# One column of shift for Bs, dt, raw, one and z: where the inputs of GpSimd's products begin in a row

## The chip, the cores and the metric

The kernel runs on one core of a Trainium2 chip. The metric is the device time of one execution in microseconds; the times are medians over several runs. The engines are PE (TensorE), DVE (VectorE), ACT (ScalarE) and POOL (GpSimd); SP issues most of the DMAs.

## The reference, cut to what matters

Four layers follow one another on a tensor of 4 x 192 x 64 x 64. The change touches the first two, which hold three "mambas": layer 0 normalises, runs two mambas over the same tokens (one of them over flipped channels) and adds their outputs; layer 1 is one mamba, a depthwise convolution and an MLP. A mamba, for each image (b) of 4096 tokens, is:

```python
xz = x @ in_w.T
xc, z = jnp.split(xz, 2, axis=-1)              # 384 channels each
xc = silu(causal depthwise convolution of xc)  # 4 taps in layer 0, 3 in layer 1
dbl = xc @ x_w.T                               # dt (12), B (16), C (16)
dt = softplus(dt @ dt_w.T + dt_b)
def step(h, inp):
    dA = exp(dt_t[..., None] * A)
    h = dA * h + (dt_t * x_t)[..., None] * B_t[:, None, :]
    y = einsum('bdn,bn->bd', h, C_t)
y = (y + D * xc) * silu(z)
return y @ out_w.T
```

The state h has 384 channels x 16 states, and the recurrence runs over the 4096 tokens. Layers 2 and 3 (a convolution with computed weights, and windows multiplied by a large structured matrix, with an MLP) are not touched.

## The kernel before, in words

Everything is fp32. A *unit* is one mamba on one tile of T = 512 tokens: layer 0 has 4 images x 8 tiles x 2 mambas = 64 units, layer 1 has 32. In SBUF a tile has 128 partitions, and a *row* here is one run of 512 columns in the free dimension. ND = 3 chunks of 128 channels make the 384.

The front of a unit (`Mamba.front`, L721) makes on PE the projection xc, the convolution and dt; ACT moves the results from PSUM into tiles. In layer 0 (`convolve`, L806) the convolution is matmuls that read `raw` at taps j = 0 to 3 (L821). In layer 1 (`summed`, `sum_taps`, L834) ACT writes three scaled copies into `raw`, `one` and `xc` (L848), and POOL adds them with two additions over 3 x 512 columns (L857: xc + raw, L859: xc + one). `one` takes the same buffer as `dt`. Then ACT makes dt (L770, softplus L777), POOL makes dtx = dt * xc into `raw` (L778, 3 x 512 columns), and SP stores dt and dtx to DRAM (L783: r_dt, r_dtx). z is projected too (ACT L743 in layer 0, L742 in layer 1), and put through silu in place (L795).

The scan handles 32 channels x 16 states at a time, in 12 tiles (k) of four rows of 512. SP loads the rows of dt and dtx back, spread over the partitions (`load`, L867: dtE, dtxE, two buffers each). For each tile:

- `product` (L896): h = dtxE * B over 4 x 512 columns. For most tiles DVE does it with B in PSUM. For the tiles called *apart* (four of twelve in the first mamba of layer 0, five in the second, three in layer 1) POOL does it, with B loaded from DRAM into `Bs` (`spread_C` L877 in layer 0, `bring_B` L890 in layer 1), and the result is `h_apart`. Both are at L903.
- ACT makes dA = exp(dt * A) row by row (`decay`, L910).
- DVE runs the recurrence on each row (`step`, L916).
- POOL multiplies by C, also loaded from DRAM (`read`, L932: h * C over 4 x 512 columns, in place but for one column).
- PE sums over the states (`sum`, L942).

At the end of every four tiles DVE takes y out of PSUM; in layer 0 it multiplies by z itself (L964), in layer 1 POOL does (`gate`, L972: xc * z over 512 columns).

The order on every engine is written out by hand: `Scans` goes through the steps, and a planner of lanes (`Behind`) puts the front of the next unit and what follows the last one between them by fixed waits and costs. It depends on nothing measured at run time. Every engine works its list in order and waits on semaphores.

Where rows begin. In the built program each of these tiles begins at a multiple of 32 bytes (8 columns) of its partition, in the kernel before and after the change. So where a row begins, modulo 8 columns, follows from the slices alone. h and h_apart already hold one column more than T: their rows begin at columns 1, 514, 1027, 1540 when POOL reads them at L932, while C begins at 0. The table gives, row by row, (start of the second input - start of the first input) modulo 4 columns, that is, modulo 16 bytes:

| line | inputs | before | after |
|---|---|---|---|
| L903 | dtxE, Bs | 0 0 0 0 | 1 1 1 1 |
| L932 | h, C | 3 2 1 0 | 3 2 1 0 |
| L778, layer 0 | dt, xc | 0 0 0 | 3 2 1 |
| L778, layer 1 | dt, xc | 0 3 2 | 3 1 3 |
| L857 | xc, raw | 0 2 0 | 1 0 3 |
| L859 | xc, one | 0 1 2 | 1 3 1 |
| L972, by chunk | xc, z | 0, 0, 0 | 1, 2, 3 |
| L1476 (rows of 64; a product's sum in layer 1's tail) | x2, strip | 3 and 1 in turn | 3 and 1 in turn |

For example, dt in layer 1 has a pitch of 513 columns before, so its rows begin at 0, 513, 1026 and those of xc at 0, 512, 1024; the difference is 0, -1, -2, or 0, 3, 2 modulo 4.

Of the kernel before, what the change touches and what calls it, by code (L numbers as in the profile page):

```python
# [14 lines left out]
F32 = mybir.dt.float32  # L15
# [12 lines left out]
ND = DI // 128  # L28
# [5 lines left out]
T = 512  # L34
# [626 lines left out]
class Mamba:  # L661
# [59 lines left out]
    def front(self, xn, first, u):  # L721


        nc, K, behind = self.nc, self.taps, self.behind
        raw = self.work.tile([128, ND, K - 1 + T], F32, name="raw", bufs=1)
        if first:
            nc.gpsimd.memset(self.halo, 0.0)
        nc.gpsimd.tensor_copy(raw[:, :, 0 : K - 1], self.halo[:, :, : K - 1])  # L728

        def projected(e):  # L730
            ps = behind.bank([128, T], "ps_in")
            for k in range(2):
                nc.tensor.matmul(  # L733
                    ps, self.in_w[:, k, bass.ts(e, 128)], xn[:, k, :], start=(k == 0), stop=(k == 1)
                )
            return ps

        def project(e, to):
            ps = projected(e)
            if e >= ND and self.z_b is not None:  # L740
                bias = self.z_b[:, e - ND : e - ND + 1]
                return behind.later(lambda: nc.scalar.activation(to, ps, AF.Identity, bias=bias), name="z")  # L742
            return behind.later(lambda: nc.scalar.copy(to, ps))  # L743

        if self.summed:
            yield from self.sum_taps(raw, projected, u)
        else:
            yield from self.convolve(raw, project, u)
        xc = u["xc"]
        nc.scalar.activation(xc, xc, AF.Silu)  # L750
        yield Piece(2.6, bank=True, wait=3 if self.summed else 4, after=u["dbl_free"])
        ps = behind.bank([KX, T], "ps_x")
        for d in range(ND):
            nc.tensor.matmul(ps, self.x_w[:, d, :], xc[:, d, :], start=(d == 0), stop=(d == ND - 1))  # L754
        dbl = u["dbl"] = self.work.tile([KX, T], F32, name="dbl", bufs=2 if self.summed else 1)
        h = behind.later(lambda ps=ps: nc.scalar.copy(dbl, ps), name="x")
        halves = []
        for d in range(ND):
            yield Piece(0.85, bank=True, after=[h], wait=(1 if d else 3) if self.summed else (0 if d else 3))
            if d == 0:  # L760
                bc = u["bc"] = self.dram.tile([2 * NS, T], F32, name="r_bc", bufs=3)
                nc.sync.dma_start(bc, dbl[RK : RK + 2 * NS, :])
                dt = self.work.tile([128, ND, 1 + T if self.summed else T], F32, name="dt", bufs=1)
                dt = dt[:, :, :T]
                dtx = raw[:, :, K - 1 :]
            ps = behind.bank([128, T], "ps_dt")
            nc.tensor.matmul(ps, self.dt_w[:, bass.ts(d, 128)], dbl, start=True, stop=True)  # L767
            halves.append(
                behind.later(
                    lambda d=d, ps=ps: nc.scalar.activation(  # L770
                        dt[:, d, :], ps, AF.Identity, bias=self.dt_b[:, d : d + 1]
                    ),
                    name="dt",
                )
            )
        yield Piece(after=halves, burst=True, act=4.1)
        nc.scalar.activation(dt, dt, AF.Softplus)  # L777
        nc.gpsimd.tensor_tensor(dtx, dt, xc, ALU.mult)  # L778
        rows = []
        for i, v in enumerate((dt, dtx)):  # L780
            yield Piece(wait=1 + i)
            r = self.dram.tile([DI, T], F32, name=("r_dt", "r_dtx")[i], bufs=3)
            nc.sync.dma_start(r.rearrange("(c p) t -> p c t", p=128), v)  # L783
            rows.append(r)
        yield Piece(1.7, bank=True, after=u["z_free"], wait=0)
        u["rows"] = rows
        z = u["z"] = self.work.tile([128, ND, T], F32, name="z", bufs=2)
        made = []
        for d in range(ND):
            if d:  # L790
                yield Piece(1.7, bank=True, wait=0)
            made.append(project(ND + d, z[:, d, :]))

        def silu():
            nc.scalar.activation(z, z, AF.Silu)  # L795
            u["silu"] = True
            yield Piece()

        said = Piece(after=made, burst=True, act=4.1)
        if self.summed:  # L800
            behind.add(4, silu(), said)
        else:
            yield said
            yield from silu()
# [29 lines left out]
    def sum_taps(self, raw, projected, u):  # L834

        nc, behind = self.nc, self.behind
        halves = []
        for d in range(ND):
            yield Piece(1.7, bank=True, after=u["xc_free"], wait=AHEAD.get(f"w_in{d}", 0))
            if d == 0:  # L840
                xc = u["xc"] = self.last.tile([128, ND, T], F32, name="xc", bufs=self.xcs)
                one = self.work.tile([128, ND, 1 + T], F32, name="one", tag="dt", bufs=1)
                nc.gpsimd.tensor_copy(one[:, :, 0:1], self.halo[:, :, 2:])
            ps = projected(d)
            for j, o in enumerate((raw[:, d, 2:], one[:, d, 1:], xc[:, d, :])):

                def tap(o=o, ps=ps, d=d, j=j):
                    nc.scalar.activation(  # L848
                        o, ps, AF.Identity, scale=self.conv_w[:, d, j : j + 1], bias=self.tap_b[:, d, j : j + 1]
                    )  # L850

                h = behind.later(tap, bank=(j == 2), more=j, name="tap")
            halves.append(h)
        yield Piece(after=halves, wait=2)
        nc.gpsimd.tensor_copy(self.halo[:, :, :2], raw[:, :, T:])
        nc.gpsimd.tensor_copy(self.halo[:, :, 2:], one[:, :, T:])
        nc.gpsimd.tensor_tensor(xc, xc, raw[:, :, :T], ALU.add)  # L857
        yield Piece(wait=2)
        nc.gpsimd.tensor_tensor(xc, xc, one[:, :, :T], ALU.add)  # L859
        yield Piece(burst=True, wait=2, act=4.1)  # L860
# [16 lines left out]
    def spread_C(self, u, o):  # L877

        both = [("Bs", 0, 1)] if any(k % 2 == o for k in self.shared) and not self.summed else []
        both.insert(len(both) if self.summed else 0, ("C", NS, 1 if self.summed else 2))  # L880
        for n, at, bufs in both:
            if n == "C" and self.summed:
                yield Piece(wait=4)
            v = self.work.tile([128, T], F32, name=f"{n}{o}", bufs=bufs)
            rows = u["bc"][at + 8 * o : at + 8 * o + 8, :]
            self.nc.sync.dma_start(v, rows.unsqueeze(0).broadcast_to([16, 8, T]))
            u[n, o] = v
            yield Piece()

    def bring_B(self, u, o):  # L890
        v = self.work.tile([128, T], F32, name="Bs", bufs=1)
        rows = u["bc"][8 * o : 8 * o + 8, :]
        self.nc.sync.dma_start(v, rows.unsqueeze(0).broadcast_to([16, 8, T]))
        u["Bs", o] = v
# [224 lines left out]
def two_mambas(tc, x, gb_ap, m_ins, ex_aps, out, at_first):  # L1119
# [3 lines left out]
    with ExitStack() as ctx:  # L1123
# [105 lines left out]
        for n, u in enumerate(units):  # L1229
            following = units[n + 1] if n + 1 < len(units) else None  # L1230

            def before(i, n=n, u=u, following=following):
                if i == 0 and following:
                    load(following)
                    last = [units[n - 1]["added"]] if n else []
                    behind.add(3, norm(following, last), Piece(wait=3))
                if following:
                    behind.add(1, front(following, i), Piece(after=[following["normed"]], wait=2))

            for i in range(2):  # L1240
                stream.append(
                    (
                        mambas[i],
                        u[i],
                        u["t"] == 0,
                        lambda i=i, before=before: before(i),
                        (lambda u=u: behind.add(2, back(u), Piece())) if i else (lambda: None),
                    )
                )
# [64 lines left out]
def mamba_block(tc, x, p96, p96_ap, p128, p128_ap, m_in, ex_aps, out, sums, following):  # L1314
# [4 lines left out]
    with ExitStack() as ctx:  # L1319
# [193 lines left out]
        def before(n):  # L1513
            if n + 1 < len(units):
                behind.add(1, front(units[n + 1]), Piece())
            if n + 2 < len(units):
                behind.add(1, norm(units[n + 2]), Piece(1.7, bank=True, after=[units[n + 2]["loaded"]]))
# [857 lines left out]
```

## Time and profile before

| | us |
|---|---|
| median of 3 runs | 9663.74 (9659.62 to 9670.88) |
| the profiled execution | 9663.24 |
| its span, first to last instruction | 9661.5 |
| PE busy | 8021.0 (83%) |
| DVE busy | 8580.3 (89%) |
| ACT busy | 6529.2 (68%) |
| POOL busy | 7624.1 (79%) |

The profile is of one execution; its own time is 1.7 us over its span and 0.5 us under the median. Layer 0 takes about the first 4950 us, layer 1 the time to about 8000, and layers 2 and 3 the rest. Busy times count an engine's instructions, not its waits. An idle time is put down to whoever ended it.

### The profile page before, as it was taken

How to read it: one execution, taken by the hardware profiler on the slowest of the kernel's cores; microseconds unless marked ns; L12 is line 12 of the kernel's file. 1: busy time of each engine (PE TensorE's matmuls, PEld its weight loads, DVE VectorE, ACT ScalarE, POOL GpSimd, SP SyncE). 2: the span in 40 equal slices, each digit the busy share in tenths (PEclk: the TensorE clock that was granted, in tenths of full speed). 3: DMA queues.
4: the chain of work that ended last, by engine and by line, in shares of the span. 5: the costliest groups of instructions: out<-in, count | busy, mean ns of one | idle time of the engine just before them, and what ended most of it. 6: DMA issues, size and time to landing. Idle time of an engine off the chain costs nothing. (4 is left out here: it accounts for less than half of the span.)

```text
span 9661.5 us, 96673 instructions
## 1 busy us (share of the span) xinstructions
PE 8021.0 (83%) x30440; PEld 3446.7 (36%) x30440; DVE 8580.3 (89%) x7515; ACT 6529.2 (68%) x10008; POOL 7624.1 (79%) x3008
## 2 busy tenths in 40 slices
PE   6877777777777777777756899999999998799998
PEld 2323222222323232222212333333333333566666
DVE  7999999999999999999995999999999996666752
ACT  5677777777777777777754678777777874354543
POOL 6999999999999999999995899999999992011100
PEclk8888888888888888888876799999999998899999
DMA  7777777777777777777765666777677762322210
GB/s 186 192 202 198 205 203 206 199 201 202 201 203 202 204 199 207 201 199 202 204 178 142 179 183 181 187 190 188 179 188 190 189 180 46 83 56 67 66 42 22
DMA packets 1034253, 1630.81 MB, mean 169 GB/s; under 512 B 252500, under 2 KB 285608, under 8 KB 1033224
## 3 DMA queue, kind: packets, MB, share of 16 engines
q1 hardware_dynamic: 1032736, 1621.30, 63.2%
q8 instruction: 240, 3.93, 0.2%
q10 hardware_dynamic: 1000, 3.30, 0.1%
q14 instruction: 277, 2.27, 0.1%
HBM read 1404.83 MB, written 219.41 MB: 168 GB/s over the span
## 5 line engine op out<-in xcount | busy, mean ns | idle before, releaser
L910 ACT ACTIVATE dA<-dtE,m_A 128x512 f32<-128x512 f32 x4608 | 3108.2, 687 | 1347.2 <-DVE h L916 1127.3
L916 DVE TENSOR_TENSOR_SCAN h<-dA,m_state,h 128x512 f32<-128x512 f32 x3072 | 3729.6, 1266 | 167.7 <-ACT dA L910 102.0
L932 POOL TENSOR_TENSOR h<-h,C 128x2048 f32<-128x2048 f32 x768 | 3203.2, 4175 | 286.5 <-DVE h L916 157.1
L916 DVE TENSOR_TENSOR_SCAN h_apart<-dA,m_state,h_apart 128x512 f32<-128x512 f32 x1536 | 1851.3, 1260 | 64.2 <-ACT dA L910 36.9
L903 DVE TENSOR_TENSOR h<-dtxE,B 128x2048 f32<-128x2048 f32 x768 | 1735.6, 2260 | 70.6 <-DMA dtxE<-r_dtx 67.8
L903 POOL TENSOR_TENSOR h_apart<-dtxE,Bs 128x2048 f32<-128x2048 f32 x384 | 1741.7, 4536 | 49.0 <-DMA Bs<-r_bc 23.3
L932 POOL TENSOR_TENSOR h_apart<-h_apart,C 128x2048 f32<-128x2048 f32 x384 | 1601.8, 4171 | 47.1 <-DVE h_apart L916 45.3
L942 PE MATMUL y<-h,gather 128*32 128x512 f32 x6144 | 949.5, 698 | 231.1 <-DVE xc L964 140.0
L1768 POOL TENSOR_TENSOR d<-d,rs 128x512 f32<-128x512 f32 x64 | 84.9, 1326 | 1258.7 <-DVE rs L1763 1258.7
L733 PE MATMUL ps_in<-xT,m_in_w 96*128 96x512 f32 x1536 | 873.8, 711 | 101.1 <-ACT z L743 49.4
L942 PE MATMUL y<-h_apart,gather 128*32 128x512 f32 x3072 | 503.1, 733 | 335.4 <-POOL h_apart L932 325.5
L821 PE MATMUL ps_conv<-raw,m_conv 128*128 128x512 f32 x1536 | 692.1, 596 | 6.6 <-POOL raw L728 6.6
L733 PEld LDWEIGHTS ps_in<-xT,m_in_w 96*128 96x128 f32 x1536 | 323.2, 227 | 729.6 <-issue 394.9
L1203 PE MATMUL ps_out<-m_pack,xc 128*128 128x192 f32 x1536 | 332.1, 368 | 248.4 <-DVE xc L964 183.0
L1452 PE MATMUL ps_dw<-strip,dw 96*96 96x512 f32 x1152 | 529.7, 606 | 0.0
L754 PE MATMUL ps_x<-xc,m_pack 128*68 128x512 f32 x576 | 391.4, 836 | 99.3 <-ACT xc L750 92.7
L910 ACT ACT_TABLE_LOAD x343 | 440.1, 1283 | 14.6 <-DMA dtE<-r_dt 8.5
L767 PE MATMUL ps_dt<-dbl,m_dt_w 68*128 68x512 f32 x576 | 318.6, 664 | 143.1 <-ACT dt L770 72.2
L821 PEld LDWEIGHTS ps_conv<-raw,m_conv 128*128 128x128 f32 x1536 | 288.1, 190 | 393.1 <-issue 376.9
L1978 PE MATMUL unit<-xn,sed 64*128 64x256 f32 (+3 forms) x2944 | 405.5, 383 | 8.8 <-DVE d L1740 5.1
L942 PEld LDWEIGHTS y<-h,gather 128*32 128x32 f32 x6144 | 133.3, 114 | 776.1 <-issue 519.7
L778 POOL TENSOR_TENSOR raw<-dt,xc 128x1536 f32<-128x1536 f32 x96 | 325.6, 3391 | 99.9 <-ACT dt L777 98.2
(208 smaller groups left out, 11660.2 us busy)
## 6 DMA issues: line engine op xcount, KB each, us to landing
dtE<-r_dt SPq DMA_DIRECT2D x2304, 256.0 KB, 5.4
dtxE<-r_dtx SPq DMA_DIRECT2D x2304, 256.0 KB, 4.4
r_dt<-dt SPq DMA_DIRECT2D x96, 768.0 KB, 4.0
r_dtx<-raw SPq DMA_DIRECT2D x96, 768.0 KB, 6.0
Bs<-r_bc SPq DMA_DIRECT2D x224, 256.0 KB, 5.4
C<-r_bc SPq DMA_DIRECT2D x192, 256.0 KB, 7.1
x<-x SPq DMA_DIRECT2D x64, 384.0 KB, 3.6
img<-x SPq DMA_DIRECT2D x28, 512.0 KB, 8.1
```

Of the source, the lines that this page charges most:

```text
L733: nc.tensor.matmul(ps, self.in_w[:, k, bass.ts(e, 128)], xn[:, k, :], start=(k == 0), stop=(k == 1))
L754: nc.tensor.matmul(ps, self.x_w[:, d, :], xc[:, d, :], start=(d == 0), stop=(d == ND - 1))
L778: nc.gpsimd.tensor_tensor(dtx, dt, xc, ALU.mult)
L821: nc.tensor.matmul(ps, self.conv[:, d, j, :], raw[:, d, j : j + T], start=(j == 0), stop=(j == K - 1))
L903: engine.tensor_tensor(h[:, :, self.more :], u["rows", k // 2, 1], u[B, k % 2].unsqueeze(1).broadcast_to([128, 4, T]), ALU.mult)
L910: self.nc.scalar.activation(dA, u["rows", k // 2, 0][:, j, :], AF.Exp, scale=self.A[:, k, j : j + 1])
L916: self.nc.vector.tensor_tensor_scan(h[:, j, self.more :], u.pop(("dA", k, j)), h[:, j, self.more :], self.state[:, k, j : j + 1], ALU.mult ...
L932: nc.gpsimd.tensor_tensor(h[:, :, :T], h[:, :, self.more :], u["C", k % 2].unsqueeze(1).broadcast_to([128, 4, T]), ALU.mult)
L942: self.nc.tensor.matmul(u["ys"][32 * j : 32 * j + 32, :], self.ex.gather[:, i // 2, :], h[:, j, :T], start=(i == 0), stop=(i == 3 and self ...
L1203: nc.tensor.matmul(ps, u[i]["xc"][:, d, bass.ts(q, 128)], mambas[i].out_w[:, d, :], start=(i == 0 and d == 0), stop=False, skip_group_chec ...
L1452: nc.tensor.matmul(ps, dw[:, k, j, :], s[:, k, dy : dy + rows, dx : dx + HW], start=(j == 0), stop=(j == 8),)
L1978: nc.tensor.matmul(out, sed[p, int(h is not None), i ^ position(k, s), cols], xn[b, g].t[p, c, :], start=start, stop=stop,)
```

## The change

The tiles Bs, dt, raw, one and z get one more column, and all their uses begin one column further in. With the wider tiles the pitch from chunk to chunk grows by one column as well: dt from 512 to 513 in layer 0 and from 513 to 514 in layer 1, raw from 515 to 516 and from 514 to 515, one from 513 to 514, z from 512 to 513. Nothing is added, removed or reordered on any engine. Softplus (dt) in layer 0 and silu (z) in both layers now go over three rows apart from each other, where they went over one run of 1536 columns.

```diff
@@ front
-        raw = self.work.tile([128, ND, K - 1 + T], F32, name="raw", bufs=1)
+        raw = self.work.tile([128, ND, K + T], F32, name="raw", bufs=1)[:, :, 1:]
...
-                dt = self.work.tile([128, ND, 1 + T if self.summed else T], F32, name="dt", bufs=1)
-                dt = dt[:, :, :T]
+                dt = self.work.tile([128, ND, 2 + T if self.summed else 1 + T], F32, name="dt", bufs=1)
+                dt = dt[:, :, 1 : 1 + T]
...
-        z = u["z"] = self.work.tile([128, ND, T], F32, name="z", bufs=2)
+        z = u["z"] = self.work.tile([128, ND, 1 + T], F32, name="z", bufs=2)[:, :, 1:]
@@ sum_taps
-                one = self.work.tile([128, ND, 1 + T], F32, name="one", tag="dt", bufs=1)
+                one = self.work.tile([128, ND, 2 + T], F32, name="one", tag="dt", bufs=1)[:, :, 1:]
@@ spread_C
-            v = self.work.tile([128, T], F32, name=f"{n}{o}", bufs=bufs)
+            v = self.work.tile([128, T + (n == "Bs")], F32, name=f"{n}{o}", bufs=bufs)
+            v = v[:, 1:] if n == "Bs" else v
@@ bring_B
-        v = self.work.tile([128, T], F32, name="Bs", bufs=1)
+        v = self.work.tile([128, 1 + T], F32, name="Bs", bufs=1)[:, 1:]
```

## The prediction

> **What bounds the kernel now.** I read the busy times by stage first, because the page's shares average over layers that have different limits. The first stretch below lies within layer 0 (two mambas), the second within layer 1 (one mamba with its MLP). Columns: start and end, length, then busy us of PE, PEld, DVE, ACT, POOL, the granted TensorE clock, the DMA share and GB/s.
>
> ```profile
> 200.00:4750.00 4550.00, 3514.47 (x11812) 1301.07 (x11804) 4403.35 (x3420) 3271.51 (x5551) 4339.66 (x1262) 0.84 0.75 202
> 5150.00:7800.00 2650.00, 2458.73 (x8326) 928.83 (x8327) 2545.30 (x2064) 2034.94 (x2663) 2468.41 (x1299) 0.94 0.70 185
> ```
>
> In layer 0 DVE is busy 96.8% and POOL 95.4%; in layer 1 it is 96.0% and 93.1%. DVE is the bound, POOL is close behind it, so a faster POOL can win only what DVE idles. After 8150 us POOL has almost nothing to do with the changed lines; that end stays as it is.
>
> Next, the POOL groups by form, first those within 0 to 4900 us, then those within 4960 to 8300 us. Columns: shapes, count, busy us, mean ns of one, idle before.
>
> ```profile
> L932 POOL TENSOR_TENSOR h<-h,C 128x2048 f32<-128x2048 f32 x463 | 1928.6, 4172 | 135.4 <-DVE h L916 88.7 <-DMA dtxE<-r_dtx 41.2 <-PE y L942 2.2
> L903 POOL TENSOR_TENSOR h_apart<-dtxE,Bs 128x2048 f32<-128x2048 f32 x278 | 1260.5, 4534 | 34.8 <-DMA Bs<-r_bc 23.3 <-DMA dtxE<-r_dtx 4.3 <-PE y L942 3.9
> L778 POOL TENSOR_TENSOR raw<-dt,xc 128x1536 f32<-128x1536 f32 x63 | 217.2, 3448 | 65.8 <-ACT dt L777 65.7
> ```
>
> ```profile
> L903 POOL TENSOR_TENSOR h_apart<-dtxE,Bs 128x2048 f32<-128x2048 f32 x103 | 467.6, 4540 | 14.2 <-issue 12.0 <-POOL m_state L927 2.2
> L972 POOL TENSOR_TENSOR xc<-xc,z 128x512 f32<-128x512 f32 x96 | 122.0, 1270 | 0.0
> L778 POOL TENSOR_TENSOR raw<-dt,xc 128x1536 f32<-128x1536 f32 x32 | 104.9, 3279 | 33.9 <-ACT dt L777 32.4 <-DVE h_apart L916 1.6
> L857 POOL TENSOR_TENSOR xc<-xc,raw 128x1536 f32<-128x1536 f32 x32 | 104.7, 3271 | 1.5 <-ACT xc L848 1.5
> L859 POOL TENSOR_TENSOR xc<-xc,one 128x1536 f32<-128x1536 f32 x32 | 99.0, 3093 | 0.1
> L1476 POOL TENSOR_TENSOR x<-x,strip 96x512 f32<-96x512 f32 x64 | 74.6, 1185 | 2.9 <-ACT x L1472 2.8
> ```
>
> The reader is to see that one operation (two fp32 inputs from SBUF) on one size takes different times: 4172 against 4534 for 2048 columns; 3448, 3279, 3271 and 3093 for 1536. L778 changes its time between the layers with no change but the pitch of dt (512, then 513). So where the rows start matters.
>
> Last, the waits of DVE and of the DMA queue (SP) within 200 to 4750 us: us in total, times, longest.
>
> ```profile
> DVE h L916 <- ACT dA L910: 46.9, 42, 3.8
> DVE h_apart L916 <- ACT dA L910: 29.4, 36, 2.6
> DVE h_apart L916 <- POOL h_apart L903: 25.4, 33, 1.3
> ```
>
> ```profile
> SPq L867 <- DVE h L903: 1172.8, 321, 11.0
> SPq L867 <- POOL h_apart L903: 363.5, 115, 8.5
> ```
>
> POOL's product L903 is the direct reason for 25.4 us of DVE's idle time, and 115 times it is what frees a dtxE buffer last, before SP may load the next one.
>
> **What a row costs POOL.** Let d be the start of the second input's row minus that of the first, modulo 4 columns (16 bytes); the table ahead gives d for each row. Solving the rows:
> - L903 has four rows at d=0, L778 in layer 0 three: 4536 - 3448 = 1088 ns for a row at d=0, and 4536 - 4 x 1088 = 184 ns fixed. L972 (one row at d=0) should then take 1272; it takes 1270.
> - L859 has d = 0, 1, 2: (3093 - 184 - 1088) / 2 = 910 ns for a row at d=1 or 2.
> - L857 (0, 2, 0): 184 + 2 x 1088 + 910 = 3270; measured 3271. So d=2 is 910, and by L859 d=1 too.
> - L778 in layer 1 (0, 3, 2): with d=3 at 1088 it is 3270; measured 3279. So d=3 is slow.
> - L932 (3, 2, 1, 0): 184 + 2 x 1088 + 2 x 910 = 4180; measured 4172. L1476 (3 and 1 in turn, 512 columns in all): 184 + 544 + 455 = 1183; measured 1185.
>
> Two levels (1088 for d = 0 and 3, 910 for d = 1 and 2) fit all seven rows within 9 ns. That the cause is the 16 bytes is my inference; the fit is from the rows.
>
> **The change, part by part.** The order of instructions on every engine and what each waits for stay as they are; only places move.
> - L903 goes from d=0 to d=1 in all four rows: 184 + 4 x 910 = 3824, so 712 ns less, 384 times: 273 us of POOL's time, 205 of it in layer 0 (288 products).
> - L778 in layer 0: (0, 0, 0) becomes (3, 2, 1): 184 + 1088 + 2 x 910 = 3092, so 356 less, 64 times: 23 us.
> - L972: d becomes 1, 2, 3 for the three chunks: 178 less in two of three: 64 x 178 = 11 us.
> - L778 in layer 1 (3, 1, 3), L857 (1, 0, 3) and L859 (1, 3, 1) keep their number of slow rows: nothing. L932 is not touched.
>
> POOL's busy time: 7624 - 307 = 7317 us.
>
> [...]
>
> **Costs beside it.** ACT writes raw, one, dt and z one column further: L848 writes raw (2 columns in) in 775 ns, one (1 in) in 769, xc (0) in 770, so nothing. Softplus and silu now run over three separate rows instead of one of 1536: L777 takes 1484 in layer 0 (one run) and 1485 in layer 1 (pitch 513), so nothing. PE reads raw at the same four places modulo 4 as before (taps 0 to 3, now 1 to 4), DVE reads z one column in as its scans read h: nothing, and 6 ns per instruction as the spread of L848 would be lost in DVE's idle time. The store r_dt reads dt 4 bytes in: it lands after 3.9 us in layer 0 (aligned) and 4.0 in layer 1, where two rows of three already start 4 and 8 bytes off; r_dtx, 12 bytes off, takes 5.9. Bounds -2.0 to +2.0 us per store; I take 0, by the nearest row, the same store in layer 1. No row shows a load into a place 4 bytes in (Bs). Bs lands in 5.6 us in layer 0, C in 8.0: bound +2.4. It is hidden: a Bs load issued at 1019.48 is first read at 1037.99, one issued at 6523.68 at 6547.46. I take 0; without that cover it is 2.4 us on 224 loads.
>
> **What of the 307 us lies on the path.** I followed the trace back from DVE's last instruction before 4940 us to 398 us, step by step as in part 4 of the page (to what released an instruction, or to the one before it). L903 holds 411.6 us of those 4541, in 91 places, and L778 0.5. From 7990 back to 5200 us L903 holds 31.7 and L972 21.4. Shortened by 712/4536, and L972 by two thirds of 178/1272: 64.6 + 5.0 + 2.0 = 72 us. With the same order and all else as long as before, no more can be won than what this chain loses, since the chain itself stays a path. The floor is DVE's direct wait for L903: 33 waits of 0.77 us on average, of which 712 ns each go: 23 us. Between 23 and 72 I take 50: DVE's own idle time holds it (146.6 us within 200 to 4750, of which 103 in gaps over 200 ns), but a dtxE buffer that POOL frees 0.7 us sooner is often held next by DVE's L903 (321 waits). So 9663.2 - 50 = 9613 us for the profiled execution, which stands 0.5 us below the median of the runs (9663.7): the forecast is 9613 for that too.
>
> **Rivals.**
> - *DVE is the bound and takes nothing.* Each 0.7 us that POOL gains is lost to DVE's next product or to ACT's exponentials, which DVE waits for longer (76 us). For: DVE 96.8% busy. Against: 25.4 us are direct. 9645 to 9664. The case that L903 stays at 4536, because a second input costs what it costs wherever it starts, ends here too, at 9663; against it stand L932 and L859. [...]
> - *Any different start gives what L932 has*, 4174: 362 ns less in place of 712, so 12 to 37 us on the path; 9639. Against: L859 and L932 don't fit one price for all.
> - *More than the chain.* Earlier free buffers also bring loads forward and free PE, which waits for POOL's h_apart and holds up ACT; then the gaps over 200 ns go, 103 us in layer 0 and some 50 in layer 1: 9510 to 9590.
> - *Slower: the stores.* If dt's odd start makes r_dt land 2.0 us later, as r_dtx does, the loads of dtE behind it in SP's queue are late, and ACT's exponentials with them: up to 96 x 2.0 = 192 us, 70 if it counts only where SP is seen to wait for the r_dtx store (35 times). It decides from 0.5 us per store (50 us over 96). Against: the row of layer 1, 4.0. With the 50 won: 9683 to 9805.
>
> **How the numbers follow.** Forecast (9590 to 9640) 0.55; half price 0.10; more than the chain 0.12; DVE takes it 0.16, of which 0.03 that L903 stays as it is; slower 0.07. A measurement of this kernel can tell about 0.2% (19 us) from no change. Faster by more: 0.55 + 0.10 + 0.12 = 0.77; within: 0.16; slower: 0.07. The range 9560 to 9662 takes in the forecast, the half price, most of the third and part of the fourth case. The two bounds of Bs and the stores beyond it hold less than the 2 in 10 left out.
>
> **What would show it.** L903 at 3824 (4174 by the half price, 4536 if the start does not matter for it); L778 at 3092 in layer 0 and near 3270 in layer 1; L972 at 1094 or 1272 by chunk; L857 and L859 as before, though none of their inputs begin at the same place. DVE's wait for L903 gone; SP's waits for it fewer; r_dt landing at 3.9 to 4.0. Wrong if DVE's busy time per instruction grows, or if r_dt or Bs land later and ACT waits for dtE.

## The result, and the profile after

| | before | after |
|---|---|---|
| median | 9670.14 us (6 runs) | 9607.00 us (6 runs, 9600.79 to 9610.68) |
| ratio | | 0.9933, 95% interval 0.9921 to 0.9946 |
| span of the profiled execution | 9661.5 | 9607.6 |
| layer 0, DVE's first to last scan | 4990.5 | 4953.9 |
| layer 1, the same | 2825.2 | 2811.7 |
| after DVE's last scan | 1667.2 | 1667.3 |
| POOL busy | 7624.1 | 7315.1 |

The kernel became 0.67% faster. The kernel before was measured again beside the changed one, so its median is 9670 us here and not 9664. The three spans of the layers show where the time went: 37 us in layer 0, 14 in layer 1, nothing in layers 2 and 3. They come from the two profiled executions, which lie 54 us apart; the medians lie 63 us apart. Lines below the change have moved by one: L903 is now L904, L916 L917, L972 L973.

The busy times in the two stretches shown before (us of PE, PEld, DVE, ACT, POOL, then clock, DMA share and GB/s):

```profile
200.00:4750.00 4550.00, 3554.13 (x11898) 1299.16 (x11897) 4441.33 (x3451) 3295.95 (x5608) 4173.99 (x1274) 0.83 0.77 204
5150.00:7800.00 2650.00, 2493.84 (x8464) 942.93 (x8465) 2578.75 (x2092) 2062.42 (x2703) 2429.88 (x1324) 0.95 0.70 186
```

POOL's share in layer 0 falls from 95.4% to 91.7%, DVE's rises from 96.8% to 97.6%: more of DVE's work fits into the same time. Next the POOL groups by form, within 0 to 4900 us and within 4960 to 8250 us (count, busy us, mean ns, idle before):

```profile
L904 POOL TENSOR_TENSOR h_apart<-dtxE,Bs 128x2048 f32<-128x2048 f32 x280 | 1067.9, 3814 | 59.0 <-PE y L943 27.0 <-DMA Bs<-r_bc 23.7 <-issue 4.4
L778 POOL TENSOR_TENSOR raw<-dt,xc 128x1536 f32<-128x1536 f32 x64 | 197.6, 3087 | 73.0 <-ACT dt L777 73.0
```

```profile
L904 POOL TENSOR_TENSOR h_apart<-dtxE,Bs 128x2048 f32<-128x2048 f32 x101 | 385.1, 3813 | 17.5 <-issue 15.8 <-POOL m_state L928 1.6
L973 POOL TENSOR_TENSOR xc<-xc,z 128x512 f32<-128x512 f32 x96 | 110.6, 1152 | 0.0
L778 POOL TENSOR_TENSOR raw<-dt,xc 128x1536 f32<-128x1536 f32 x32 | 104.6, 3270 | 45.8 <-ACT dt L777 44.6 <-DVE h_apart L917 1.2
L857 POOL TENSOR_TENSOR xc<-xc,raw 128x1536 f32<-128x1536 f32 x32 | 104.5, 3266 | 3.1 <-ACT xc L848 3.1
L859 POOL TENSOR_TENSOR xc<-xc,one 128x1536 f32<-128x1536 f32 x32 | 98.8, 3088 | 0.1
```

The reader is to see that L904 fell from 4534 to 3814 ns and L778 in layer 0 from 3448 to 3087, while L778 in layer 1, L857 and L859 stayed where they were although none of their inputs begin at the same place any more. The waits of DVE within 200 to 4750 us:

```profile
DVE h L917 <- ACT dA L911: 39.7, 63, 1.6
DVE h_apart L917 <- ACT dA L911: 25.8, 36, 3.2
DVE xc L965 <- PE y L953: 1.8, 2, 1.2
```

The line of POOL's product (25.4 us before) is gone, and the two lines of waits for ACT fell from 76.3 to 65.5 us.

### The profile page after: what moved, and what is told of

The parts are those of the page before. It is cut to its first block, busy times and chain, and to the rows that moved or that the text cites. A ratio compares the mean times of both kernels' runs of the same rounds, so it can differ in the third digit from the quotient of the medians.

```text
span 9607.6 us, 96673 instructions
## 1 busy us (share of the span) xinstructions
PE 8034.0 (84%) x30440; PEld 3437.2 (36%) x30440; DVE 8576.6 (89%) x7515; ACT 6524.6 (68%) x10008; POOL 7315.1 (76%) x3008
## 5 line engine op out<-in xcount | busy, mean ns | idle before, releaser
L917 DVE TENSOR_TENSOR_SCAN h<-dA,m_state,h 128x512 f32<-128x512 f32 x3072 | 3729.8, 1266 | 148.7 <-ACT dA L911 82.5
L933 POOL TENSOR_TENSOR h<-h,C 128x2048 f32<-128x2048 f32 x768 | 3205.4, 4175 | 484.0 <-DVE h L917 328.2
L917 DVE TENSOR_TENSOR_SCAN h_apart<-dA,m_state,h_apart 128x512 f32<-128x512 f32 x1536 | 1850.7, 1259 | 33.9 <-ACT dA L911 32.5
L904 DVE TENSOR_TENSOR h<-dtxE,B 128x2048 f32<-128x2048 f32 x768 | 1735.9, 2260 | 67.0 <-DMA dtxE<-r_dtx 65.6
L933 POOL TENSOR_TENSOR h_apart<-h_apart,C 128x2048 f32<-128x2048 f32 x384 | 1601.0, 4169 | 54.4 <-DVE h_apart L917 52.6
L904 POOL TENSOR_TENSOR h_apart<-dtxE,Bs 128x2048 f32<-128x2048 f32 x384 | 1464.4, 3814 | 76.6 <-PE y L943 27.0
L733 PE MATMUL ps_in<-xT,m_in_w 96*128 96x512 f32 x1536 | 912.0, 739 | 110.1 <-ACT z L743 50.0
L943 PE MATMUL y<-h_apart,gather 128*32 128x512 f32 x3072 | 476.1, 695 | 236.7 <-POOL h_apart L933 226.0
L1204 PE MATMUL ps_out<-m_pack,xc 128*128 128x192 f32 x1536 | 312.2, 351 | 228.8 <-DVE xc L965 183.0
L874 PE MATMUL B<-dbl,spread 68*128 68x512 f32 x512 | 349.2, 770 | 100.5 <-DVE h L904 80.4
```

The source lines that it names most:

```text
L733: nc.tensor.matmul(ps, self.in_w[:, k, bass.ts(e, 128)], xn[:, k, :], start=(k == 0), stop=(k == 1))
L874: self.nc.tensor.matmul(B, self.ex.spread[:, o, :], u["dbl"], start=True, stop=True)
L904: engine.tensor_tensor(h[:, :, self.more :], u["rows", k // 2, 1], u[B, k % 2].unsqueeze(1).broadcast_to([128, 4, T]), ALU.mult)
L917: self.nc.vector.tensor_tensor_scan(h[:, j, self.more :], u.pop(("dA", k, j)), h[:, j, self.more :], self.state[:, k, j : j + 1], ALU.mult ...
L933: nc.gpsimd.tensor_tensor(h[:, :, :T], h[:, :, self.more :], u["C", k % 2].unsqueeze(1).broadcast_to([128, 4, T]), ALU.mult)
L943: self.nc.tensor.matmul(u["ys"][32 * j : 32 * j + 32, :], self.ex.gather[:, i // 2, :], h[:, j, :T], start=(i == 0), stop=(i == 3 and self ...
```

## The experiments

Theory: a row of a POOL product is slow (1088 ns for 512 columns) where the second input starts 0 or 3 columns after the first, modulo 4, and fast (some 907) at 1 or 2; the time is won where DVE waited for POOL's product. Rivals: any other start will do; the parts beside Bs matter; what counts is the product's share of the chain followed back through the trace.

### Which part of the change it is

Bs shifted in layer 0 alone:

```diff
-            v = self.work.tile([128, T], F32, name=f"{n}{o}", bufs=bufs)
+            s = (1, 1)[o] if n == "Bs" else 0
+            v = self.work.tile([128, s + T], F32, name=f"{n}{o}", bufs=bufs)[:, s:]
```

> The kernel before with Bs shifted by one column in layer 0 alone (spread_C). Every theory has POOL's product there near 3814 ns. Theory (the gain is what POOL's product held on the path of layer 0): about 40 us faster than before, 9630 against 9670, nearly all of it ahead of the last scan of layer 0 (39.6 us there in the changed kernel). Rival (the shift of dt, raw, one and z does part of it): less than 30 us. Rival (the parts only help together, since DVE waits for whichever is last): less than 20 us.

Measured: 9639.49 against 9670.80, ratio 0.9971 (0.9961 to 0.9981), 31 us by the medians. The interval (18 to 38 us) ends just below the 40 expected, so this run alone does not exclude that the rest of the change does a part.

Bs shifted in layer 1 alone:

```diff
-        v = self.work.tile([128, T], F32, name="Bs", bufs=1)
+        v = self.work.tile([128, 1 + T], F32, name="Bs", bufs=1)[:, 1:]
```

> The kernel before with Bs shifted by one column in layer 1 alone (bring_B): 96 products at 3814 in place of 4540 ns, 70 us of POOL's time. By the chain of before, which holds 31.7 us of this product in layer 1, no more than 5 us can be won: 9665 to 9670. Rival (layer 1 wins its 14 us, as the pair of profiles shows, through this product): 9656. Rival (the 14 us are spread between executions): within 10 us either way.

Measured: 9651.66, ratio 0.9986 (0.9977 to 0.9995): 19 us by the medians, 14 by the ratio, 5 to 22 by the interval, which by itself just touches the chain's limit of 5 us. The profiles decide it. Layer 1's scans span 2807.9 us here, and between 2824.8 and 2826.1 us in the four profiles of this document in which every tile of layer 1 is as before. So the chain's limit does not hold, and its rival does: the product is worth some 17 us in layer 1. Layer 0 is less steady: with its tiles as before it takes 4990.5, 4996.7 and 5000.9 us in three profiles.

Everything but Bs (both lines of Bs as in the kernel before):

> The changed kernel with Bs back at column 0 in both layers; dt, raw, one and z stay shifted. POOL wins 23 us in L778 of layer 0 and 11 us in L973, and nothing in L857 and L859. By the chain at most 2.5 us come of it: 9668 to 9670. Rival (layer 1's 14 us come from the gate and from the front): 9656. Rival (odd starts of dt and raw cost a store or ACT something that the gain of Bs hides): slower than before by 5 us or more, with r_dt landing later than 4.0 us.

Measured: 9668.37, ratio 0.9999 (0.9990 to 1.0008): nothing, though POOL's busy time fell to 7589.2. The store r_dt lands after 3.8 us in layer 0 and 4.0 in layer 1 of the changed kernel (3.9 and 4.0 before), so it costs nothing either. The three medians add up to 53 us against 63 for the whole; their intervals (each some 9 us to either side) cover the difference. That the parts help together is not excluded, though: with Bs alone DVE still waits 5.5 us for POOL's product within 200 to 4750 us, in the whole change not at all, and layer 0 takes 4966.6 us against 4953.9.

### Is it the 16 bytes?

Bs at other columns in the kernel before; the even and odd tiles of layer 0 get names of their own:

```diff
+            s = (2, 3)[o] if n == "Bs" else 0       # the second kernel: (4, 6)
+            v = self.work.tile([128, s + T], F32, name={"C": f"C{o}", "Bs": ("Bs_even", "Bs_odd")[o]}[n], bufs=bufs)[:, s:]
...
+        v = self.work.tile([128, 5 + T], F32, name="Bs", bufs=1)[:, 5:]   # the second kernel: 7
```

> The kernel before with Bs starting at other columns: column 2 for the even tiles of layer 0 (Bs_even), 3 for the odd ones (Bs_odd), 5 in layer 1. Theory of the 16 bytes (the distance modulo 4 counts; 0 and 3 are slow, 1 and 2 fast): POOL's product takes about 3814 ns with Bs_even, 4536 with Bs_odd, 3814 in layer 1. Rival (any start other than the first input's is fast): 3814 in all three. Rival (an odd column is what counts): 4536, 3814, 3814.

> The same with column 4 for the even tiles of layer 0, 6 for the odd ones, 7 in layer 1. Theory of the 16 bytes: 4536, 3814, 4536. Rival (any other start is fast): 3814 in all three. Rival (the pattern has a period of 8 columns, 32 bytes): 4 columns differ from 0, 6 from 2 or 7 from 3 in the run before.

POOL's product by name, first with columns 2 (even), 3 (odd) and 5 (layer 1), then with 4, 6 and 7:

```profile
L904 POOL TENSOR_TENSOR h_apart<-dtxE,Bs_odd 128x2048 f32<-128x2048 f32 x160 | 725.4, 4534 | 9.4 <-issue 5.2 <-PE y L943 3.9
L904 POOL TENSOR_TENSOR h_apart<-dtxE,Bs_even 128x2048 f32<-128x2048 f32 x128 | 488.3, 3815 | 27.8 <-DMA Bs_even<-r_bc 23.5 <-DMA dtxE<-r_dtx 3.9 <-ACT dA L911 0.4
L904 POOL TENSOR_TENSOR h_apart<-dtxE,Bs 128x2048 f32<-128x2048 f32 x96 | 366.2, 3814 | 18.5 <-issue 16.4 <-POOL m_state L928 2.1
```

```profile
L904 POOL TENSOR_TENSOR h_apart<-dtxE,Bs_odd 128x2048 f32<-128x2048 f32 x160 | 610.2, 3814 | 17.2 <-PE y L943 12.6 <-issue 4.3
L904 POOL TENSOR_TENSOR h_apart<-dtxE,Bs_even 128x2048 f32<-128x2048 f32 x128 | 580.9, 4538 | 28.7 <-DMA Bs_even<-r_bc 23.7 <-ACT raw L743 5.0
L904 POOL TENSOR_TENSOR h_apart<-dtxE,Bs 128x2048 f32<-128x2048 f32 x96 | 436.5, 4547 | 14.3 <-issue 12.1 <-POOL m_state L928 2.2
```

All six are as the theory has them: 1 (the change itself), 2, 5 and 6 columns are fast (3814 or 3815 ns), 0, 3, 4 and 7 slow (4534 to 4547). Starting at another place is not enough; over the starts 0 to 7 the pattern repeats after 4 columns, and "odd" is not the rule. These two kernels ran once each, for the times of the products; the first took 9625.84 us, the second 9671.76.

Then every row made fast: all pitches a multiple of 4 columns, so that the distance is the same in every row, and starts chosen to make it 1 or 2:

```diff
# from the changed kernel
-        raw = self.work.tile([128, ND, K + T], F32, name="raw", bufs=1)[:, :, 1:]
+        raw = self.work.tile([128, ND, 4 + T], F32, name="raw", bufs=1)[:, :, 1 : K + T]
...
+                dt = self.work.tile([128, ND, 4 + T], F32, name="dt", bufs=1)
+                dt = dt[:, :, 2 : 2 + T]
+        # one likewise from column 2, z from column 1, h and h_apart [128, 4, T + 4]
...
+            s = 1 if n == "Bs" else 2               # C starts at column 2
+            v = self.work.tile([128, s + T], F32, name=f"{n}{o}", bufs=bufs)[:, s:]
```

> The changed kernel with pitches of 516 columns (a multiple of 4) for h, h_apart, dt, raw, one and z, C starting at column 2, dt and one at column 2: every row of all POOL products has its second input 1 or 2 columns after the first, modulo 4. Theory of the 16 bytes: the product with C falls from 4175 to 3814, L778 in both layers, L857 and L859 to about 2910, L973 to 1094 in all three chunks; POOL's busy time 7315 - 460 = 6855 us. In time, at most 25 us by the chain of the changed kernel (201 us of the product with C in layer 0, 47 in layer 1, of which 8.6% go), and about 15: 9592. Rival (a row's time depends on where each input starts by itself, and the product with C has its first input at column 1): the product with C stays near 4175. Rival (DVE is the bound by now): POOL's times fall and the time stays at 9607.

```profile
L933 POOL TENSOR_TENSOR h<-h,C 128x2048 f32<-128x2048 f32 x768 | 2929.0, 3814 | 821.2 <-DVE h L917 630.0 <-DMA dtxE<-r_dtx 86.4 <-PE rb L583 54.2
L778 POOL TENSOR_TENSOR raw<-dt,xc 128x1536 f32<-128x1536 f32 x96 | 279.3, 2909 | 148.1 <-ACT dt L777 145.8 <-DVE h_apart L917 2.3
L973 POOL TENSOR_TENSOR xc<-xc,z 128x512 f32<-128x512 f32 x96 | 104.9, 1093 | 0.0
L857 POOL TENSOR_TENSOR xc<-xc,raw 128x1536 f32<-128x1536 f32 x32 | 93.0, 2906 | 4.2 <-ACT xc L848 3.4
L859 POOL TENSOR_TENSOR xc<-xc,one 128x1536 f32<-128x1536 f32 x32 | 92.9, 2904 | 0.1
```

Every product took the forecast time, also the one with C, whose first input starts at column 1 and whose second at 2 (3814 ns, as with dtxE at 0 and Bs at 1): here the distance counts, not each input's own start. This is the only pair with neither row at a multiple of 4 columns; two rows that both begin at column 1, say, were not tried. POOL's busy time is 6866.0 us. Measured: 9586.74, ratio 0.9920 (0.9907 to 0.9932), 84 us faster than before and about 21 us more than the change itself (both against their own runs of before), where about 15 and at most 25 were expected.

### Where the time is won

The pair of runs with other columns held a surprise. (A tile holds 64 channels and 8 of the 16 states, not 32 channels and all 16: the even tiles have the first eight states, the odd ones the others, each with a Bs of its own.) With 128 fast products in layer 0 (even tiles) its scans span 4966.3 us, as short as with all 288 fast (4966.6); with the 160 odd ones fast, 4998.7. So I asked, product by product, which of them DVE waited for in the trace of before: within 200 to 4750 us, 28 of the 33 waits and 22.1 of the 25.4 us belong to one, tile 4 of the second mamba, which stands only two tiles after tile 2. (The 29 and 22.6 us in the expectation below take in one more wait after 4750 us.)

Bs shifted for the even tiles of the second mamba alone, and, in another kernel, for the odd tiles of both:

```diff
+            s = 1 if n == "Bs" and o == 0 and self.name == "m1" else 0    # the other: n == "Bs" and o == 1
+            v = self.work.tile([128, s + T], F32, name=f"{n}{o}", bufs=bufs)[:, s:]
```

> The kernel before with Bs shifted only for the even tiles (2 and 4) of the second mamba of layer 0: 64 of the 384 products. In the trace of before 29 of the 33 direct waits of DVE for POOL's product (22.6 of 25.4 us) are for tile 4 of the second mamba. If those waits are what the change removes in layer 0: the same gain as with all 288 products of layer 0 shifted, 20 to 31 us, 9640 to 9650 against 9670. Rival (every product on the path counts alike, so the share of the 91 places goes by 29 of 91): about 10 us. The waits of DVE for POOL's product go from 25 to some 6 us.

> The kernel before with Bs shifted only for the odd tiles of layer 0 (5, 7, 9, 11): 160 of the 384 products, 115 us of POOL's time. The chain followed back through before holds these products in 62 of its 91 places: by it as a sum, up to 44 us faster. If only DVE's direct waits count: within 10 us of before, 9660 to 9675.

DVE's waits for POOL's product within 200 to 4750 us, first with the 64 even products of the second mamba fast, then with the 160 odd ones:

```profile
DVE h_apart L917 <- POOL h_apart L904: 8.6, 19, 1.1
```

```profile
DVE h_apart L917 <- POOL h_apart L904: 22.8, 30, 1.2
```

Measured: 9639.06, ratio 0.9967 (0.9954 to 0.9979) with 64 products; 9669.35, ratio 0.9998 (0.9989 to 1.0007) with 160. Sixty-four products win all that 288 won (31 us), and 115 us of POOL's time elsewhere win nothing that can be told from noise. The traces agree. With the 64 products fast, DVE's waits for POOL's product fall by 16.8 us and layer 0's scans span 21 us less (4969.3 against 4990.5), while DVE's waits for ACT stay where they were (72.7 against 76.3 us); of the 28 waits at tile 4, 14 are left. So the gain of Bs in layer 0 hangs in the main on DVE's wait at one tile. What the products of tile 2 and tile 4 do separately was not tried.

In layer 1 DVE never waits for POOL's product directly (0 us within 5150 to 7800 us). Two paths could carry the gain: POOL's product times C, for which PE waits, or the two additions of the front (L857, L859), which stand in POOL's queue behind its products and release ACT's silu. Only the additions made fast, Bs as before:

```diff
+        s = 1 if self.summed else 0
+        raw = self.work.tile([128, ND, K - 1 + T + 2 * s], F32, name="raw", bufs=1)[:, :, s : s + K - 1 + T]
...
+                one = self.work.tile([128, ND, 4 + T], F32, name="one", tag="dt", bufs=1)[:, :, 2 : 3 + T]
```

> The kernel before with raw and one in layer 1 at a pitch of 516 columns and started so that all rows of the two additions of the front (xc + raw, xc + one) are fast: about 2910 in place of 3271 and 3093 ns, 17 us of POOL's time in all; Bs and the rest as before. If layer 1 gains because the front's additions, which stand behind POOL's products in its queue, release ACT's silu of xc earlier: some 8 to 17 us faster. Rival (layer 1 gains because PE waits less for POOL's product times C, and ACT behind PE): within 5 us of before.

Measured: 9640.93, ratio 0.9969 (0.9956 to 0.9981), 30 us (18 to 43), more than the 8 to 17 expected, from 17 us of POOL's time; the profile has the additions at 2910 and 2911 ns, and layer 1's scans at 2797.6 us. ACT's wait for the second addition within 5150 to 7800 us, in the kernels before, with Bs of layer 1 shifted, and with the additions fast:

```profile
ACT xc L750 <- POOL xc L859: 22.9, 24, 5.0
```

```profile
ACT xc L750 <- POOL xc L859: 13.8, 6, 5.0
```

```profile
ACT xc L751 <- POOL xc L860: 11.8, 6, 4.4
```

Both edits take away the same 18 waits of ACT. They also bring the time of a unit to the same value: from one unit's first scan to the next's, most units take between 87.5 and 88.8 us before, and 87.0 in most with either edit. How the product and the additions hang together can be read from POOL's timeline in the kernel before (start, length):

```profile
6516.61 4.55 POOL L903 TENSOR_TENSOR h_apart<-dtxE,Bs 128x2048 f32<-128x2048 f32 x1
6521.13 4.16 POOL L932 TENSOR_TENSOR h<-h,C 128x2048 f32<-128x2048 f32 x1
6525.26 1.26 POOL L972 TENSOR_TENSOR xc<-xc,z 128x512 f32<-128x512 f32 x1
6527.16 3.27 POOL L857 TENSOR_TENSOR xc<-xc,raw 128x1536 f32<-128x1536 f32 x1
6530.39 4.18 POOL L932 TENSOR_TENSOR h<-h,C 128x2048 f32<-128x2048 f32 x1
6534.54 3.08 POOL L859 TENSOR_TENSOR xc<-xc,one 128x1536 f32<-128x1536 f32 x1
```

POOL works here without a break (copies and a memset of 0.14 to 0.28 us fill the rest), so what the product saves reaches the additions whole. Counted from the unit's first scan, the second addition ends after 32.76 us before (the middle of 23 units), after 32.04 with Bs shifted and after 32.23 with the additions fast.

So layer 1 wins through the front: POOL ends its additions sooner, ACT does not stand still at the silu with everything queued behind it, and the exponentials come in time (DVE's wait for them between 5220 and 7940 us goes from 51.7 to 38.0 us with Bs shifted). The rival (PE's wait) is not needed as the first cause, as the additions alone do it; but PE's wait for POOL's product times C fell with either edit (from 20.1 to 5.0 us with Bs shifted, to 10.8 with the additions fast), and what it adds was not tested. Why the additions win more than the 17 us they save stays open. The granted TensorE clock (as a share of full speed) moved with them: 0.886 to 0.888 in these five runs. In the fifteen runs of the kernel before that stand beside them, the three at a clock of 0.882 took 9678 to 9679 us and the two at 0.886 took 9656 and 9662. Whether the clock is a cause or goes with a shorter time, the runs don't tell, so differences of some 10 us between two kernels' medians are not certain to be the edit's.

### Using the room that POOL gained

One more product of the first mamba moved from DVE to POOL, in the changed kernel and in the one with all rows fast:

```diff
-                ((2, 5, 8, 11), (2, 4, 7, 9, 11))[i], xcs=4,
+                ((2, 4, 7, 9, 11), (2, 4, 7, 9, 11))[i], xcs=4,
```

> The changed kernel with five instead of four of the twelve products of the first mamba of layer 0 on POOL (tiles 2, 4, 7, 9, 11, as the second mamba has it): 32 products of 2260 ns leave DVE (72 us) and 32 of 3814 come to POOL (122 us). If the idle time that the change gives POOL is there to be used and DVE is the bound: 30 to 60 us faster than the changed kernel, 9550 to 9577. Rival (POOL becomes the bound again, as it is busy 91.7% in layer 0 and would be 94.4%): 9597 to 9617, no gain.

> The kernel with all rows fast (9587) and the same fifth product of the first mamba of layer 0 on POOL. POOL has more room there than in the changed kernel, so nearly all of DVE's 72 us can be won: 9525 to 9550. Rival (what DVE waits for is ACT's exponentials and not its own work): 9570 to 9587.

Measured: 9575.15, ratio 0.9906 (0.9889 to 0.9922), and 9561.71, ratio 0.9892 (0.9877 to 0.9907) against 9667.25. The first is 32 us below the change (29 when each is set against its own runs of before), at the lower edge of the 30 to 60 expected. The second, the fastest of all, is 106 us below the kernel before, but misses its 9525 to 9550: it lies 25 us below the kernel with all rows fast, between the forecast and the rival. DVE's waits within 200 to 4750 us, in the kernel with all rows fast and then in the same with the fifth product:

```profile
DVE h L917 <- ACT dA L911: 44.4, 65, 2.2
DVE h_apart L917 <- ACT dA L911: 17.0, 20, 3.2
```

```profile
DVE h L917 <- ACT dA L911: 78.5, 93, 1.5
DVE h_apart L917 <- ACT dA L911: 25.7, 50, 1.0
DVE h_apart L917 <- POOL h_apart L904: 0.2, 1, 0.2
```

POOL is out of the way (0.2 us); DVE now waits for ACT's exponentials, 104 us against 61 without the fifth product. My reading is that a product on DVE (2260 ns) gave ACT time for its other work, and that ACT is late where the product is gone. That is an argument from the waits and was not tested.

## Why the prediction was right

- **9613 forecast, 9607 measured**: -0.5% against -0.67%, or 50 us against 63. The baseline moved as well, from 9664 to 9670.
- **The price of a row** was right within 10 ns for each product: L903 to 3824 (3814 measured), L778 in layer 0 to 3092 (3087), in layer 1 3270 (3270), L972 to 1094 in two chunks of three (1152 as the mean of all), L857 and L859 unchanged, POOL busy 7317 (7315). The two levels and the period of 4 columns, inferred from seven rows, held at six further starts.
- **The costs taken at nothing** were nothing: with all shifts but Bs the time did not move, r_dt lands as before (3.8 us in layer 0 against 3.9, 4.0 in layer 1), and Bs at 6.1 us in layer 0 (5.6 before) and 5.2 in layer 1 (5.1 before). POOL stands still for Bs once, at the very start, 23.7 us against 23.3 before.
- **Where it lies on the path** was right as a sum and wrong in its parts, so that the sum came out is in part luck. I took 50 us between a floor of 23 (DVE's direct waits, layer 0) and a ceiling of 72 (the chain: 65 in layer 0, 7 in layer 1), and no sum led to the 50. Layer 0 gave 31 with Bs alone, near the floor: the direct waits were the real thing. Of the chain's 91 places 29 are tile 4's, and 21 of these lead straight to DVE's scan. The other 62, of odd tiles, were worth nothing that could be measured; in 43 of them the chain goes on to SP's next load (L867) into a freed buffer, in 19 to POOL's next product. That other work was as late there is my reading, not shown.
- **The ceiling of layer 1** failed. It gave 14 to 19 us against 5 for its product, so "no more can be won than what this chain loses" does not hold there. The chain holds the product in 7 places of layer 1 and the two additions in 16 units, 100 us. In 14 of the 17 places where it comes to the gate, it steps back over a waiting instruction in POOL's queue (at L856) to ACT's copy of `one`. But the timeline above has POOL at work right up to the gate, with L932 and L903, and everything from the product on came 0.7 us sooner when the product was shortened. So the product lay on POOL's path in those units too, and the way I followed the trace back passed it by. The 18 waits of ACT for the additions stood in the list of waits all along.
- **The rivals**: the half price fell (3814, not 4174). DVE did not swallow the gain, although it is the bound, because one of its waits was for POOL (25.4 us within 200 to 4750 us before, none after). The stores did not slow (r_dt above; r_dtx 6.0 us in layer 0 against 5.9, 6.5 in layer 1). The case "more than the chain" came true for layer 1 alone, and through the front, which it did not name.

## What to carry to other kernels

When one operation takes several times for one size, write the starts of its rows beside the times and solve for a price per row; here that gave the time of each product to within 10 ns before the change was run. Choose the pitch as well as the start: where the pitches of the two inputs differ by an odd number of columns, as with 513 and 512, the distance takes all four values in four rows, and two of the four were slow here, so some rows are slow whatever the start (the product with C: 4175 ns with h at a pitch of 513, 3814 at 516 with C from column 2). "Not the same place" is not the rule (Bs at column 3: 4534 ns). For what a faster engine is worth, go through the direct waits for it, instance by instance and also for what stands behind it in its queue, before summing its share of a chain: 64 products were worth 31 us and 160 others nothing.

## What the runs showed of the hardware

POOL's two-input operation on fp32 had a price per row of 512 columns that, in all pairs tried here, goes by the distance of the inputs' starts modulo 16 bytes: 1088 ns at 0 or 12 bytes, some 907 at 4 or 8 ((3814 - 184) / 4), beside some 184 ns for the instruction (4536 - 4 x 1088). The three are solved from the times of whole instructions. With every row fast, products and additions took the same (2909 ns for the product of L778, 2906 and 2904 for the additions of L857 and L859), and so did two starts of the output: 3817 ns where it starts at column 1 (POOL's product into h_apart, L904), 3814 where it starts at column 0 (the product with C into h, L933). 12 bytes are as slow as the same place: 4534 ns with Bs at column 3, 4536 at column 0. No run here shows why 12 bytes fall on the slow side, nor why the pattern repeats after 16 bytes.
